# Running the products and the convolution of v ahead of q and k in the first stage of a two-layer attention kernel

## The chip, the core and the metric

The kernel runs on one core of a Trainium2 chip. A core has five engines with an instruction stream each: TensorE (PE in the profile, its weight loads PEld), VectorE (DVE), ScalarE (ACT), GpSimd (POOL) and SyncE (SP), which issues the DMAs of this kernel's first two stages. Each stream runs its instructions in the order in which the kernel was built, and semaphores make one stream wait for another. The metric is the device time of one execution, in microseconds (us).

## What is computed

The input x has 4 images of 192 channels and 128 x 128 pixels, in fp32. Two layers follow each other. The first is channel attention (8 heads of 24 channels, q and k divided by their norms over the pixels) with a gate:

```python
qkv = dwconv3x3(conv1x1(x, w_qkv), w_dw)
q, k, v, l = jnp.split(qkv, 4, axis=1)
attn = softmax(einsum('bhcn,bhdn->bhcd', q, k) * temperature)
out = einsum('bhcd,bhdn->bhcn', attn, v)
pooled = mean(l, axis=(2, 3))
t = conv1x1(relu(conv1x1(pooled, w_fc1, b_fc1)), w_fc2, b_fc2)
L = t * sigmoid(t)
out = conv1x1(L + out + x, w_proj) + L
```

The second is a dilated local attention: x gains a depthwise 3x3 convolution and a bias, a 1x1 convolution gives q, k and v, six heads of 32 channels attend to 9 neighbours at a dilation of 1, 2 or 3, and a 1x1 convolution follows. Its code is not touched by the change.

## The kernel before

There are three stages, one after the other.

**First stage** (`project`, `plan_projection`). The images go in pairs, and a pair in 32 blocks of four rows, so there are 64 blocks n. A block's x (`xt`, 128 partitions by 3 by 512 elements: 128 channels of each image, and the 64 remaining channels of both) is loaded by three DMAs. Its 1x1 convolution gives q and k in three tiles of 128 channels (`mt` 0 to 2) and v in tile 3 and a `shared` tile for the last 64 channels of both images. A tile of q and k takes full-array products (L293) and then products of the 64 remaining channels on two halves of the array (L298); v takes L426, L431, L303 and, on half the columns, L307. The results stand in `pu`, six buffers of PSUM, until ScalarE copies them out: q and k to `us` (six buffers, L311), which a DMA stores to `qk_dram` (L315); v to `vboth` and `ring` (L322), which hold three blocks of rows. Every third block some rows are copied again behind a ring's end (L172).

The depthwise convolution of v is done on these rings. For the first 128 channels ScalarE makes the centre tap into `pa` (one buffer, L333), and VectorE adds eight taps to it (L340), of which the last writes `v_False`. For the shared tile ScalarE makes nine scaled copies (centre L333, and `side`, three buffers, L352), which GpSimd sums (L363). Both are stored to DRAM (L370, L373). VectorE also sums every block of x for the gate (`totals`, L377), and GpSimd copies its edge columns (`edges`, L381).

The order of all this is made by hand and by a small planner (`Schedule`). Each operation is added with an engine, a rank, a cost and what it must follow; `order()` plays the plan through, and on every free engine takes the ready operation of the lowest rank, with a small penalty where a product would change the shape of the array. `hold` says how long a buffer is taken. Ranks are in blocks: rank n is the time of block n. SyncE's DMAs are planned the same way, and its stream, too, is fixed in that order: a store that waits for its data holds back all DMAs behind it. The weights of later stages are given ranks from 8 on.

**Second stage** (`channel_attention`). For each of 8 heads, first for q and then for k (`convolved`, `which` 0 and 1), the depthwise convolution is made by products with band matrices (L576) in six steps of four channels. A step loads `band` (three buffers, L555; GpSimd completes it, L563 and L566) and `u` (four buffers, four DMAs each from `qk_dram`, L558). ScalarE copies the results out of `pc` (L585), VectorE takes their statistics (L589). Then come the products of q and k (L648) and the rest of the head. At the end of each of the six steps `step()` is called (L590), which runs the next piece of pending work on small tiles: first the two gates (`gate_bias`, five pieces each for a pair of images), then the softmax of the heads done. The gate's products go to a PSUM buffer, and the head's results to a buffer in SBUF, that lie where the first stage had its own.

**Third stage** (`second_pass`): the product with the mixed weights, and the second layer. It takes most of the time.

The change touches `plan_projection` (ranks in `plan_products` and `plan_conv`), one line of `project`, and the call of `step()` in `convolved`.

Of the kernel before, what the change touches and what calls it, by code (L numbers as in the profile page):

```python
# [24 lines left out]
RING = 12  # L25
# [161 lines left out]
FULL, COLS, ROWS, QUADS = "128x128", "128x64", "64x128", "128x32"  # L187
# [64 lines left out]
def project(tc, x, load, other_loads, sums, qk_dram, v_dram, v2_dram):  # L252

    nc = tc.nc
    with ExitStack() as ctx:
        wts = ctx.enter_context(tc.tile_pool(name="p1w", bufs=1))
        wx, wx2, wv2, dwv = (load(wts, n) for n in ("wx", "wx2", "wv2", "dwv"))
        stage = Stage(ctx, tc, "p1", dict(xt=4, us=6, v=3, v2=3, side=3, ring=1), dict(pu=6, pa=1))  # L260
        rings = stage.pools["ring"]
        vboth = rings.tile([128, RING + SPARE, 2, W + 2], F32, tag="vboth", name="vboth")
        ring = [vboth[:, :, 0], vboth[:, :, 1]]
        ring.append(rings.tile([128, RING + SPARE, W + 2], F32, tag="ring2", name="ring2"))
        for r in ring:
            nc.gpsimd.memset(r[:, :, 0 : W + 2 : W + 1], 0.0)
        plan_projection(nc, stage, x, wx, wx2, wv2, dwv, vboth, ring, sums, qk_dram, v_dram, v2_dram)
        for i, run in enumerate(other_loads):
            stage.schedule.add("SP", 8 + i, 0.5, run)
        stage.run(tc)  # L270


def plan_projection(nc, stage, x, wx, wx2, wv2, dwv, vboth, ring, sums, qk_dram, v_dram, v2_dram):
# [113 lines left out]
        nc.vector.tensor_reduce(sums[n // NB][2][:, :, to : to + 1], tiles["xt", n][:, :, of : of + W], AX.X, ALU.add)  # L387

    def plan_products(n):
        load_op = add("SP", n - 1.5, 0.5, (loads, n), latency=6.0)  # L390
        users = []
        shared = add("PE", n + 0.52, 0.86, (shared_tile, n, 0), [load_op], FULL)
        users.append(shared)
        for mt in range(4):
            t = n + 0.5 * (mt // 2) + 0.01 * (mt % 2)
            first, second = (first_half_v, second_half_v) if mt == 3 else (first_half, second_half)
            args = (n,) if mt == 3 else (n, mt)
            a = add("PE", t, 1.72, (first, *args), [load_op], FULL)
            b = add("PE", t + 0.2, 0.86, (second, *args), [a], ROWS)
            users += [a, b]  # L400
            if mt == 3:
                continue
            evs = [add("ACT", t + 0.25, 0.56, (qk_evict, n, mt, im), [b]) for im in range(2)]
            for ev in evs:
                hold("pu", a, ev)
            hold("us", evs[0], add("SP", t + 0.3, 0.3, (qk_store, n, mt), evs, latency=5.0))
            evs[1]["first"].append(evs[0])
        last = add("PE", n + 0.75, 0.9, (shared_tile, n, 1), [shared], COLS)
        users.append(last)
        for m in range(3):  # L410
            ev = add("ACT", n + 0.8, 0.56, (v_evict, n, m), [last if m == 2 else b])
            stage.fill("u", m, n, RING, ev)
            stage.repeat(ring, "u", m, n, RING, n + 0.83)
            hold("pu", shared if m == 2 else a, ev)
        users.append(add("DVE", n + 0.5, 1.7, (totals, n), [load_op]))
        users += [add("POOL", n + 0.3 * k, 0.2, (edges, n, k), [load_op]) for k in range(3)]
        if n % NB == 0:
            users.append(add("DVE", n, 0.5, (edge_row, n, 2, 0), [load_op]))
        if n % NB == NB - 1:
            users.append(add("DVE", n, 0.5, (edge_row, n, 0, PX - W), [load_op]))  # L420
        hold("xt", load_op, *users)
# [9 lines left out]
            mm(tiles["pu", n, 3, im], w, tiles["xt", n][HALVES[im], 2, :], start=False, stop=True)  # L431

    def plan_conv(n):
        prev = first = add("ACT", n + 2, 1.2, (centre, n, False), latency=0.3)
        for j, t in enumerate(AROUND):
            prev = add("DVE", n + 2 + (j + 0.9) / 8, 1.22, (tap, n, t, j == 7), [prev])
            for m in range(2):
                stage.read("u", m, n, t // 3 - 1, prev)
        for m in range(2):
            stage.read("u", m, n, 0, first)  # L440
        hold("pa", first, prev)
        store = add("SP", n + 3.0, 0.3, (v_store, n, False), [prev], latency=5.0)
        hold("v", prev, store)
        prev = first = add("ACT", n + 2, 0.7, (centre, n, True))
        stage.read("u", 2, n, 0, first)
        for j, t in enumerate(AROUND):
            sd = add("ACT", n + 2 + (j + 0.4) / 8, 0.68, (side, n, t))
            stage.read("u", 2, n, t // 3 - 1, sd)
            prev = add("POOL", n + 2 + (j + 0.9) / 8, 1.26, (side_sum, n, t), [sd, prev])
            hold("side", sd, prev)  # L450
        store = add("SP", n + 3.0, 0.3, (v_store, n, True), [prev], latency=5.0)
        hold("v2", first, store)

    for n in range(2 * NB + 1):
# [64 lines left out]
def channel_attention(tc, d, load, qk_dram, mix1, mix2, band_p, u_p, gates):  # L519
# [7 lines left out]
    with ExitStack() as ctx:  # L527
# [18 lines left out]
        def convolved(hd, which, pool):  # L546
            c0 = which * C + hd * CH0
            full = pool.tile([128, B, W // 4, CH0, 4], F32, tag="conv", name=f"conv{which}_{hd}")
            stats = st.tile([128, B, CH0, 6], F32, tag=f"stats{which}", name=f"stats{which}_{hd}")
            for c2 in range(0, half, 2):  # L550
                band = band_p.tile([128, 2, 2, 3, G], F32, tag="band", name=f"band{which}_{hd}_{c2}")
                u = u_p.tile([128, 2, 2, B * W], F32, tag="u", name=f"u{which}_{hd}_{c2}")
                for e in range(2):
                    first = c0 + e * half + c2
                    nc.sync.dma_start(band[HALVES[e], e], d["bands"][:, first : first + 2])  # L555
                    for r in range(2):
                        to = (r + e) % 2 * G
                        nc.sync.dma_start(  # L558
                            u[to : to + G, e],
                            qk_dram[first : first + 2, r * G : (r + 1) * G].rearrange("c h b w -> h c (b w)"),  # L560
                        )
                for e in range(2):
                    nc.gpsimd.tensor_copy(band[HALVES[1 - e], e], band[HALVES[e], e])  # L563
                    for r in range(2):
                        cut = G - 1 - r * (G - 1)
                        nc.gpsimd.memset(band[HALVES[(r + e) % 2], e, :, :, cut : cut + 1], 0.0)  # L566
                for c in range(2):
                    pcs = [
                        ps_c.tile([128, B, W], F32, tag="pc", name=f"pc{which}_{hd}_{c2}_{c}_{e}") for e in range(2)
                    ]  # L570
                    for dx in (1, 0, 2):
                        to, of = shifted(dx)
                        for e in range(2):
                            for r in range(2):
                                at = slice((r + e) % 2 * G, (r + e) % 2 * G + G)
                                nc.tensor.matmul(  # L576
                                    pcs[e][r * G : (r + 1) * G, :, to],
                                    band[at, e, c, dx, :],
                                    u[at, e, c, :].rearrange("p (b w) -> p b w", w=W)[:, :, of],
                                    start=dx == 1,  # L580
                                    stop=dx == 2,
                                )
                    for e in range(2):
                        ch = e * half + c2 + c
                        nc.scalar.copy(full[:, :, :, ch, :], pcs[e].rearrange("p b (v w) -> p b v w", w=4))  # L585
                        for b in range(B):

                            of = pcs[e][:, b, :] if hd or which else full[:, b, :, ch, :]
                            nc.vector.bn_stats(stats[:, b, ch, :], of)  # L589
                step()  # L590

            flat = stats.rearrange("p b c s -> p (b c) s")
            sq = st.tile([128, B, CH0], F32, tag=f"sq{which}", name=f"sq{which}_{hd}")
            sqf = sq.rearrange("p b c -> p (b c)")
            nc.vector.tensor_mul(flat[:, :, 1:5:3], flat[:, :, 1:5:3], flat[:, :, 1:5:3])
            nc.vector.tensor_add(sqf, flat[:, :, 1], flat[:, :, 4])
            nc.vector.tensor_scalar_mul(sqf, sqf, float(W // 2))
            nc.vector.tensor_add(sqf, sqf, flat[:, :, 2])
            nc.vector.tensor_add(sqf, sqf, flat[:, :, 5])
            return full, sq  # L600
# [775 lines left out]
```

## Time and profile before

| | us |
|---|---|
| median of 3 runs (4567.59 to 4570.33) | 4569.71 |
| profiled execution | 4564.56 |
| its span | 4562.7 |
| first stage, to TensorE's last product of it | about 853 |
| second stage | to about 1630 |

The busy time of each engine in stretches of 100 us from the first stage's steady part to its end and into the second (TensorE, VectorE, ScalarE, GpSimd, and the granted clock of TensorE):

| stretch | TensorE | VectorE | ScalarE | GpSimd | clock |
|---|---|---|---|---|---|
| 600 to 700 | 100.00 | 88.84 | 87.71 | 78.85 | 1.00 |
| 700 to 800 | 100.00 | 91.83 | 87.66 | 81.41 | 1.00 |
| 800 to 900 | 81.88 | 81.51 | 72.65 | 67.28 | 0.91 |
| 900 to 1000 | 100.00 | 52.00 | 31.49 | 17.32 | 1.00 |

A row of the profile's groups or of its timeline names the line of the kernel, the engine, the operation, what it writes and reads, and how often; the bracket behind it gives the idle time before it and what ended that. Matmuls are pipelined and their ends are modelled, so the distance from one start to the next says more than their durations.

### The profile page before, as it was taken

The page shows a single profiled execution, that of the slowest core. Times are in us where ns is not written, and L with a number is a line of the kernel's source. Part 1 is how long each engine was busy: PE and PEld are TensorE (multiplying, and loading weights), DVE is VectorE, ACT ScalarE, POOL GpSimd, SP SyncE. Part 2 cuts the span into 40 slices and gives each one's busy share as a digit, 9 for nine tenths or more (in the row PEclk, how much of TensorE's full clock was granted, in tenths as well). Part 3 has the DMA queues.
Part 4 walks back from the last instruction along what each step waited for, and adds up shares of the span by engine and source line. Part 5 has one row for each costly group of instructions (what it writes and reads, how often), then busy time and mean ns, then how long its engine had stood idle before and what let it go on. Part 6 is the DMA issues. An engine that isn't in the chain of part 4 may idle for free.

```text
span 4562.7 us, 64190 instructions
## 1 busy us (share of the span) xinstructions
PE 4416.8 (97%) x20608; PEld 1602.8 (35%) x20608; DVE 3907.4 (86%) x5556; ACT 2506.2 (55%) x4794; POOL 3354.2 (74%) x3343
## 2 busy tenths in 40 slices
PE   9999999899999989999999999999999999999986
PEld 3333333345544532333333333333333333333321
DVE  7998889755455547899999999999999999999996
ACT  7888888633233345555555555555555555555531
POOL 6777788611111115888989999998998989999897
PEclk9999999999999989999999999999999999999997
DMA  8777787678677734443444443444434444344311
GB/s 271 241 242 232 244 256 242 192 164 178 150 167 169 167 89 97 99 99 97 101 98 93 105 103 91 106 96 101 101 90 108 98 100 101 92 109 99 78 44 28
DMA packets 483951, 608.93 MB, mean 133 GB/s; under 512 B 136528, under 2 KB 318364, under 8 KB 483616
## 3 DMA queue, kind: packets, MB, share of 16 engines
q1 hardware_dynamic: 464160, 504.94, 40.6%
q0 software_dynamic: 19456, 99.89, 11.3%
q8 instruction: 166, 2.72, 0.3%
q14 instruction: 169, 1.38, 0.1%
HBM read 277.72 MB, written 201.33 MB: 105 GB/s over the span
## 4 chain that ended last, share of the span: by engine, by line
PE 71%; DVE 14%; issue 6%; POOL 6%; DMA 2%; ACT 1%; POOLq 0%; SPq 0%; DVEq 0%; ACTq 0%
PE pc L576 11%; PE ph L803 9%; PE pu L293 7%; PE ex L1146 6%; PE sc L1022 6%; DVE prod L1011 5%; DVE term L1152 5%; POOL acc L1155 4%; PE pu L298 4%; PE gram L648 4%; PE po L1168 3%; PE po L1164 3%; PE pkv L945 3%; PE pu L426 2%; PE q L1000 2%
## 5 line engine op out<-in xcount | busy, mean ns | idle before, releaser
L1155 POOL TENSOR_TENSOR acc<-acc,term 128x512 f32<-128x512 f32 x1536 | 1977.4, 1289 | 211.9 <-DVE term L1152 135.5
L1152 DVE TENSOR_TENSOR term<-ex,vring 128x512 f32<-128x512 f32 (+2 forms) x1596 | 1007.3, 661 | 65.8 <-PE ex L1146 38.9
L1011 DVE TENSOR_TENSOR prod<-q,kring 128x1536 f32<-128x1536 f32 (+1 forms) x600 | 1008.3, 1686 | 31.7 <-ACT kring L963 13.8
L363 POOL TENSOR_TENSOR v_True<-v_True,side 128x512 f32<-128x512 f32 (+1 forms) x512 | 647.9, 1267 | 168.8 <-ACT side L352 141.1
L340 DVE SCALAR_TENSOR_TENSOR pa<-vboth,dwv,pa 128x1024 f32<-128x1024 f32 (+1 forms) x448 | 574.3, 1282 | 76.8 <-ACT pa L333 54.3
L1146 PE MATMUL ex<-e_sb,spread 108*128 108x512 bf16 x1728 | 596.2, 387 | 45.2 <-DVE acc L1152 21.3
L858 DVE SCALAR_TENSOR_TENSOR pa<-hboth,posw,pa 128x1024 f32<-128x1024 f32 (+1 forms) x384 | 489.5, 1275 | 59.0 <-ACT pa L846 45.1
L576 PE MATMUL pc<-u,band 64*64 64x508 f32 (+1 forms) x4608 | 517.5, 590 | 1.4 <-ACT ring L322 1.4
L563 POOL COPY band<-band 64x384 f32<-64x384 f32 x192 | 96.7, 504 | 561.3 <-DMA band<-in_bands 484.8
L1022 PE MATMUL sc<-prod,pick 128*32 128x512 f32 x3456 | 484.1, 607 | 4.1 <-DVE e L1079 2.8
L589 DVE BATCH_NORM_STATS2 stats<-pc 128x6 f32<-128x128 f32 x1440 | 303.3, 283 | 141.3 <-ACT conv L585 141.1
L1146 PEld LDWEIGHTS <-spread 108*128 108x128 bf16 x1728 | 149.0, 98 | 723.7 <-issue 692.2
L945 PE MATMUL pkv<-y,wkv 128*128 128x512 f32 x768 | 389.0, 618 | 8.1 <-ACT kring L958 2.5
L882 ACT ACTIVATE side<-hring,posw 128x512 f32<-128x512 f32 x512 | 335.2, 710 | 102.1 <-DMA side<-side 79.8
L803 PE MATMUL ph<-xv,mix 128*128 128x512 f32 (+1 forms) x1024 | 383.4, 606 | 5.4 <-DMA xv<-v_dram 4.9
L585 ACT COPY conv<-pc 128x512 f32<-128x512 f32 x384 | 211.4, 587 | 295.4 <-PE pc L576 288.8
L293 PE MATMUL pu<-xt,wx 128*128 128x512 f32 x768 | 365.3, 612 | 7.6 <-DMA xt<-in_x 7.6
L352 ACT ACTIVATE side<-ring,dwv 128x512 f32<-128x512 f32 (+1 forms) x512 | 350.6, 736 | 15.1 <-POOL v_True L363 14.3
L958 ACT COPY kring<-pkv 64x512 f32<-64x512 f32 x384 | 223.2, 581 | 221.7 <-PE pkv L948 210.5
L576 PEld LDWEIGHTS pc<-u,band 64*64 64x64 f32 x4608 | 188.4, 133 | 302.3 <-issue 282.1
L1171 ACT COPY o<-po 128x512 f32<-128x512 f32 x192 | 106.2, 588 | 304.5 <-PE po L1164 203.8
L958 ACT COPY vring<-pkv 64x512 f32<-64x512 f32 x384 | 223.4, 582 | 45.4 <-PE pkv L948 35.7
(164 smaller groups left out, 5961.0 us busy)
## 6 DMA issues: line engine op xcount, KB each, us to landing
qk_dram<-us SPq DMA_DIRECT2D x192, 512.0 KB
u<-qk_dram SPq DMA_DIRECT2D x384, 256.0 KB
side<-side POOLq DMA_DIRECT2D x124, 768.0 KB, 5.8
xt<-in_x SPq DMA_DIRECT2D x64, 512.0 KB
v_dram<-v_False SPq DMA_DIRECT2D x64, 512.0 KB
xv<-in_x SPq DMA_DIRECT2D x128, 256.0 KB
xv<-v_dram SPq DMA_DIRECT2D x128, 256.0 KB
out<-o SPq DMA_DIRECT2D x128, 256.0 KB
```

The lines of the kernel that those rows point to most:

```text
L293: mm(pu, wx[:, mt * 128 : (mt + 1) * 128], tiles["xt", n][:, im, :], start=True, stop=False)
L340: nc.vector.scalar_tensor_tensor(by_row(to[:, o : o + length]), by_row(vboth[:, at : at + length, :, t % 3 : t % 3 + W]), dwv[:, 0, t : t ...
L363: nc.gpsimd.tensor_add(v[:, rows, :], v[:, rows, :], z[:, rows, :])
L576: nc.tensor.matmul(pcs[e][r * G : (r + 1) * G, :, to], band[at, e, c, dx, :], u[at, e, c, :].rearrange("p (b w) -> p b w", w=W)[:, :, of], ...
L803: mm(to, w[:, cols], tiles["xv", n, j, im], start=j == 0, stop=j == 2)
L858: nc.vector.scalar_tensor_tensor(by_row(to[:, o : o + length]), by_row(hboth[:, at : at + length, :, t % 3 : t % 3 + W]), posw[:, 0, t : t ...
L945: mm(rows3(tile_of("pc", key)), w, tiles["y", n, im], start=True, stop=False)
L1011: nc.vector.tensor_mul(to[:, :, px].rearrange("p t (r w) -> p t r w", w=W), q.unsqueeze(1).to_broadcast([128, 3, *q.shape[1:]]), three,)
L1022: mm(sc[quad * 32 : (quad + 1) * 32, :], pick[:, QR - 4 * row : QR - 4 * row + 32], tiles["prod", n, k // NT, k % NT // 3][:, k % 3, :], s ...
L1146: mm(rows3(tile_of("ex", ("ex", n, g, t))), spread[:, t, :], e_sb, start=True, stop=True)
L1152: nc.vector.tensor_mul(rows3(to[:, px]), rows3(ex[:, px]), win)
L1155: nc.gpsimd.tensor_add(tiles["acc", n, g], tiles["acc", n, g], tiles.pop(("term", n, g, t)))
```

## The change

In the ranks of the first stage the load of x moves from n - 1.5 to n - 4.0 and gets seven buffers instead of four. v's products (tile 3 and the shared tile), their evictions and the convolution of v move three blocks earlier: products from n + 0.5 to n - 2.5, convolution from n + 2 to n - 1. Tile 0 of q and k moves from n to n - 0.5, tile 1 from n + 0.01 to n, tile 2 from n + 0.5 to n + 0.01. The totals and the edges keep their ranks. In the second stage the steps of the first head's q no longer call `step()`, so the gates' pieces begin with its k.

```diff
--- before.py
+++ after.py
@@ -257,7 +257,7 @@
     with ExitStack() as ctx:
         wts = ctx.enter_context(tc.tile_pool(name="p1w", bufs=1))
         wx, wx2, wv2, dwv = (load(wts, n) for n in ("wx", "wx2", "wv2", "dwv"))
-        stage = Stage(ctx, tc, "p1", dict(xt=4, us=6, v=3, v2=3, side=3, ring=1), dict(pu=6, pa=1))
+        stage = Stage(ctx, tc, "p1", dict(xt=7, us=6, v=3, v2=3, side=3, ring=1), dict(pu=6, pa=1))
         rings = stage.pools["ring"]
         vboth = rings.tile([128, RING + SPARE, 2, W + 2], F32, tag="vboth", name="vboth")
         ring = [vboth[:, :, 0], vboth[:, :, 1]]
@@ -387,12 +387,12 @@
         nc.vector.tensor_reduce(sums[n // NB][2][:, :, to : to + 1], tiles["xt", n][:, :, of : of + W], AX.X, ALU.add)
 
     def plan_products(n):
-        load_op = add("SP", n - 1.5, 0.5, (loads, n), latency=6.0)
+        load_op = add("SP", n - 4.0, 0.5, (loads, n), latency=6.0)
         users = []
-        shared = add("PE", n + 0.52, 0.86, (shared_tile, n, 0), [load_op], FULL)
+        shared = add("PE", n - 2.48, 0.86, (shared_tile, n, 0), [load_op], FULL)
         users.append(shared)
         for mt in range(4):
-            t = n + 0.5 * (mt // 2) + 0.01 * (mt % 2)
+            t = n + (-0.5, 0.0, 0.01, -2.49)[mt]
             first, second = (first_half_v, second_half_v) if mt == 3 else (first_half, second_half)
             args = (n,) if mt == 3 else (n, mt)
             a = add("PE", t, 1.72, (first, *args), [load_op], FULL)
@@ -405,12 +405,12 @@
                 hold("pu", a, ev)
             hold("us", evs[0], add("SP", t + 0.3, 0.3, (qk_store, n, mt), evs, latency=5.0))
             evs[1]["first"].append(evs[0])
-        last = add("PE", n + 0.75, 0.9, (shared_tile, n, 1), [shared], COLS)
+        last = add("PE", n - 2.25, 0.9, (shared_tile, n, 1), [shared], COLS)
         users.append(last)
         for m in range(3):
-            ev = add("ACT", n + 0.8, 0.56, (v_evict, n, m), [last if m == 2 else b])
+            ev = add("ACT", n - 2.2, 0.56, (v_evict, n, m), [last if m == 2 else b])
             stage.fill("u", m, n, RING, ev)
-            stage.repeat(ring, "u", m, n, RING, n + 0.83)
+            stage.repeat(ring, "u", m, n, RING, n - 2.17)
             hold("pu", shared if m == 2 else a, ev)
         users.append(add("DVE", n + 0.5, 1.7, (totals, n), [load_op]))
         users += [add("POOL", n + 0.3 * k, 0.2, (edges, n, k), [load_op]) for k in range(3)]
@@ -431,24 +431,24 @@
             mm(tiles["pu", n, 3, im], w, tiles["xt", n][HALVES[im], 2, :], start=False, stop=True)
 
     def plan_conv(n):
-        prev = first = add("ACT", n + 2, 1.2, (centre, n, False), latency=0.3)
+        prev = first = add("ACT", n - 1, 1.2, (centre, n, False), latency=0.3)
         for j, t in enumerate(AROUND):
-            prev = add("DVE", n + 2 + (j + 0.9) / 8, 1.22, (tap, n, t, j == 7), [prev])
+            prev = add("DVE", n - 1 + (j + 0.9) / 8, 1.22, (tap, n, t, j == 7), [prev])
             for m in range(2):
                 stage.read("u", m, n, t // 3 - 1, prev)
         for m in range(2):
             stage.read("u", m, n, 0, first)
         hold("pa", first, prev)
-        store = add("SP", n + 3.0, 0.3, (v_store, n, False), [prev], latency=5.0)
+        store = add("SP", n, 0.3, (v_store, n, False), [prev], latency=5.0)
         hold("v", prev, store)
-        prev = first = add("ACT", n + 2, 0.7, (centre, n, True))
+        prev = first = add("ACT", n - 1, 0.7, (centre, n, True))
         stage.read("u", 2, n, 0, first)
         for j, t in enumerate(AROUND):
-            sd = add("ACT", n + 2 + (j + 0.4) / 8, 0.68, (side, n, t))
+            sd = add("ACT", n - 1 + (j + 0.4) / 8, 0.68, (side, n, t))
             stage.read("u", 2, n, t // 3 - 1, sd)
-            prev = add("POOL", n + 2 + (j + 0.9) / 8, 1.26, (side_sum, n, t), [sd, prev])
+            prev = add("POOL", n - 1 + (j + 0.9) / 8, 1.26, (side_sum, n, t), [sd, prev])
             hold("side", sd, prev)
-        store = add("SP", n + 3.0, 0.3, (v_store, n, True), [prev], latency=5.0)
+        store = add("SP", n, 0.3, (v_store, n, True), [prev], latency=5.0)
         hold("v2", first, store)
 
     for n in range(2 * NB + 1):
@@ -587,7 +587,8 @@
 
                             of = pcs[e][:, b, :] if hd or which else full[:, b, :, ch, :]
                             nc.vector.bn_stats(stats[:, b, ch, :], of)
-                step()
+                if hd or which:
+                    step()
 
             flat = stats.rearrange("p b c s -> p (b c) s")
             sq = st.tile([128, B, CH0], F32, tag=f"sq{which}", name=f"sq{which}_{hd}")
```

## The prediction

> **What bounds the kernel now.** I read the page first: TensorE's busy share leads, so the question for a stage is whether TensorE ever waits in it.
>
> ```profile
> span 4562.7 us, 64190 instructions
> PE 4416.8 (97%) x20608; PEld 1602.8 (35%) x20608; DVE 3907.4 (86%) x5556; ACT 2506.2 (55%) x4794; POOL 3354.2 (74%) x3343
> ```
>
> Then the timeline of TensorE at the end of the first stage. The columns are start, busy time, engine, line, operation, names, and in brackets idle time and what ended it.
>
> ```profile
> 786.92 3.70 PE L293 MATMUL pu<-xt,wx 128*128 128x512 f32 x8
> 790.55 1.99 PE L298 MATMUL pu<-xt,wx 64*128 64x512 f32 x8
> 792.47 1.98 PE L293 MATMUL pu<-xt,wx 128*128 128x512 f32 x4
> 794.38 1.13 PE L298 MATMUL pu<-xt,wx 64*128 64x512 f32 x4
> 795.44 1.98 PE L426 MATMUL pu<-xt,wx 128*128 128x512 f32 x4
> ...
> 839.97 3.70 PE L293 MATMUL pu<-xt,wx 128*128 128x512 f32 x8
> 843.60 1.99 PE L298 MATMUL pu<-xt,wx 64*128 64x512 f32 x8
> 845.52 1.98 PE L293 MATMUL pu<-xt,wx 128*128 128x512 f32 x4
> 847.34 1.88 PE L426 MATMUL pu<-xt,wx 128*128 128x512 f32 x4
> ...
> 851.92 1.08 PE L307 MATMUL pu<-xt,wx 128*64 128x512 f32 x4
> 854.46 8.12 PE L576 MATMUL pc<-u,band 64*64 64x512 f32 x72 [1.45 <-ACT ring L322]
> 878.98 0.46 PE L489 MATMUL pl<-reach,wl 128*96 128x9 f32 x2 [16.41 <-DVE v_False L340]
> ```
>
> Rows begin where the last ends: TensorE bounds the stage. The first block shown takes 13.36 us (its successor starts at 800.28), the last 12.96. The first returns to the 64-row shape once more: two extra changes of array shape, 0.40 us, 0.20 each. The products end at 852.93. Then TensorE idles 1.45 and 16.41 us, the second until VectorE's last tap of block 63. That idle is the prize. VectorE's and GpSimd's timelines show the tail:
>
> ```profile
> 857.22 9.24 DVE L340 SCALAR_TENSOR_TENSOR pa<-vboth,dwv,pa 128x1024 f32<-128x1024 f32 x7 [4.33 <-ACT pa L333]
> 869.08 8.44 DVE L340 SCALAR_TENSOR_TENSOR pa<-vboth,dwv,pa 128x1024 f32<-128x1024 f32 x7 [1.30 <-ACT pa L333]
> 877.55 1.28 DVE L340 SCALAR_TENSOR_TENSOR v_False<-vboth,dwv,pa 128x1024 f32<-128x1024 f32 x1
> ...
> 873.03 7.18 POOL L363 TENSOR_TENSOR v_True<-v_True,side 128x512 f32<-128x512 f32 x6
> ```
>
> After the last product of v, two blocks of convolution remain: VectorE ends 25.9 us later (878.83), GpSimd 27.3 (about 880.2).
>
> **What the Trainium skill says.** "TensorEngine Tiling (Array Packing)", Key Properties: changing the tiling mode drains TensorE. The trace agrees, 0.20 us a change. "TensorE: Matmul & The Clock Gate", section on the architectural detail of the array: ScalarE and VectorE are strict FIFOs, and only weight loads are pulled ahead on TensorE. It agrees: convolution products stood behind L489 for 16.41 us. "DMA: Bandwidth & Descriptors", Two DMAs through the same engine are not ordered: a dependent DMA must wait for the first one's semaphore. SyncE's waits show this, u (L558) for the q store: 1.6 us, once.
>
> **The change, part by part.** It adds no arithmetic; the built instruction order shows what moves. Times below count from the end of the last product of v, "V".
>
> *End of the stage.* Behind V the changed order still has q's and k's tiles 1 and 2 (of three, 128 channels each) of block 61 and all three of 62 and 63: three pair groups of 5.55 us (839.97 to 845.52) and two single groups of 2.97 (792.47 to 795.44), 22.6 us. VectorE's tail hangs on the eviction of v, the centre tap and 16 taps in one accumulator; nothing in it shortens, so it ends at V + 25.9. The first gate products (L489) now stand ahead of the head's products and wait for it: 25.9 - 22.6 = 3.3 us idle instead of 1.45 + 16.41 = 17.9. Gain 14.6. The 72 products that ran at 854.46 now run after it, at the same cost.
>
> SyncE is next in line. Its order puts both stores of v of block 63 ahead of the rest of u. GpSimd's tail without the two band copies that stood in it (871.27 to 873.03) is 25.5 us; evictions now mixed between `side` copies add some 0.7, so V + 26.2. Two issues take 1.1 (1.09 at 880.24), the u load 0.6, and landing 4.9 (the first x, 2.60 to 7.48): V + 32.8. TensorE needs it after the gate's 2.9 and 16 products of 0.22, at V + 32.4. Cost 0.4, from 0 (a landing of 3.9, as one x at 388.80) to 3. The other u parts follow 1.2 us apart, a tile per 5.35.
>
> *Shapes.* Of the products' rows, 369 neighbours differ in shape in the order before, 403 in the new one: pair, single and v groups interleave worse. 34 x 0.20 = 6.8 us, all on TensorE, which bounds the stage. Bounds 5 to 8.
>
> *Start.* Before, block 3 ended at 63.79; four blocks of 12.96 from 7.61 end at 59.45, so 4.3 us were lost. Now SyncE loads seven x first, and GpSimd's edge copies of all seven stand ahead of its first side sum. Block landings at 8.6, 12.2, 15.4, 18.2 put the seventh at 18.2 + 3 x 3.1 = 27.5. The first sum ends at 29.0; ScalarE, with three `side` buffers, holds its fourth and fifth copy behind the first two sums and tile 0's evictions behind those, so tile 0's first accumulator comes free at 31.2. TensorE has done three blocks of v, tile 0 of block 0 and one product of tile 1 by 25.6 (7.61 + 4.84 + 4.84 + 7.41 + 0.9) and waits until 31.3. Sums then pace ScalarE until v of block 3 ends at 43.8, where unbroken work (two v groups of 4.84, 795.44 to 800.28, two merged ones of 7.41, 845.52 to 852.93, and a pair) would end at 37.7: lost 6.1, so + 1.8. Bounds -2 (x lands faster) to + 6.
>
> *DMA behind the start.* The same bytes, three x earlier. Weights (25 small loads) and the first stores come after them on SyncE, and the slices from 50 to 100 us already ran at 292 GB/s with the engines 94% busy. x is now needed four blocks after issue, and `us` frees six deep, so this should hide; if not, a late x holds GpSimd's edge copies, then ScalarE. 0 to 5 us, I take 1.
>
> *Seven buffers of x.* 18 KB more per partition; the head's buffer over it waits for the same last tap. Nothing, or up to 1.6 us gained where x was late (388.80).
>
> *Gate.* Six calls of step() leave q for k and the next head. The same products, about 11 us with their waits, run on TensorE either way: 0, bounds -1 to + 1.
>
> Sum: -14.6 + 0.4 + 6.8 + 1.8 + 1.0 = -4.6 us against the profiled execution, 4564.56 (span 4562.7 plus 1.9 around it), giving 4560.0. The median of the runs is 5.15 above that execution, so I forecast 4569.71 - 4.6 = 4565.1.
>
> **Rivals.** Against 0.2%, 9.1 us, which is about what a measurement here can tell from no change.
>
> (a) *The lead covers everything.* The start costs no more than before, u lands in time, no x is late: -14.6 + 6.8 - 1.6 = -9.4, and with a shorter tail (conv of 61 done earlier, since totals and gate sums no longer stand in it) -11: 4559. For it: VectorE and GpSimd have slack, 12.2 us (taps 10.5, total 1.7) and 10.6 (8 sums of 1.27 and the edges) in a block of 13.2. Against: the tail was already only taps.
>
> (b) *Slower: accumulators run short in every block.* v holds three of six `pu` buffers at a group's end, and ScalarE then stands before `pa`'s centre tap (L333) until VectorE is done, with q's and k's evictions queued behind. From V, evicting v takes 1.6, the ring copies 1.5 in every third block, side, centre and two more 3.8; k's evictions come at about 7 and the next v needs their buffers at 7.4 where its group merges with q's, at 8.5 otherwise. If the centre waits over 0.5 to 1 us longer than now, TensorE loses the rest. At 0.3 us in 60 blocks that is 18 us: 4583. For it: ScalarE is 88% busy here (87.66 of 100 us at 700 to 800). Against: before has the same counts of buffers and evictions and TensorE waits 3.3 us in all. It decides from 0.23 us a block.
>
> (c) *Not what it says.* The head's start moves less than the products do, because u waits behind the v stores and the side sums end late (V + 31): the net is about 0, 4570.
>
> **How the numbers follow.** Forecast's own case 0.50 (4561 to 4569), (a) 0.20, (b) 0.17, (c) 0.13. Faster by over 0.2% is (a), 0.20; slower (b), 0.17; the rest 0.63. The range 4556 to 4578 takes in (c), most of (a) and the upper bounds of start, backlog and landing (+ 4.2, + 4, + 2.6), and leaves out most of (b).
>
> **What would show it.** Right: TensorE idle at L489 of 2 to 5 us on VectorE's last tap; the products ending some 9 us later than 852.93; a first long wait near 27 to 31 us; more of the rows with two 64-row groups. Wrong: TensorE waits on ScalarE spread over the whole stage (b), a wait on u's DMA of over 3 us (c), or an idle below 1 us at L489 with the products ending before 860 (a).

## The result

| | median us | lowest to highest | runs |
|---|---|---|---|
| kernel before | 4567.28 | 4564.25 to 4570.58 | 20 |
| changed kernel | 4575.35 | 4568.62 to 4577.77 | 20 |

The changed kernel takes 1.0017 times as long, with a 95% interval of 1.001 to 1.0024. It is 8.1 us slower where 4.6 us less was forecast. The two profiled executions differ by a similar amount, 9.8: 4574.39 against 4564.56, spans 4572.6 and 4562.7. The changed kernel's page has:

```profile
span 4572.6 us, 64232 instructions
PE 4438.0 (97%) x20608; PEld 1605.8 (35%) x20608; DVE 3910.5 (86%) x5556; ACT 2511.8 (55%) x4795; POOL 3359.3 (73%) x3343
```

TensorE has as many instructions as before, but 21.2 us more of busy time (4416.8 before). About half of that was forecast, as 14.6 us less idle time in a total only 4.6 us shorter. The rest of the loss does not appear as idle time either. A product of k's convolution is shown with 586 to 641 ns, and in an unbroken step the products overlap so far that 48 take 5.35 us. When data is late fewer overlap: the row becomes longer (6.37 us below), and TensorE counts as busy all through it.

The timeline of TensorE in the changed kernel, from the end of the first stage through head 0, to the start of head 1's products of q and k. The gram product is L649 here and was L648 before.

```profile
859.56 1.99 PE L298 MATMUL pu<-xt,wx 64*128 64x512 f32 x8
864.73 0.34 PE L489 MATMUL pl<-reach,wl 128*96 128x9 f32 x2 [3.18 <-DVE v_False L340]
...
867.40 38.19 PE L576 MATMUL pc<-u,band 64*64 64x512 f32 x288
907.07 6.57 PE L576 MATMUL pc<-u,band 64*64 64x512 f32 x48 [1.49 <-DMA cut<-qk_dram]
914.25 6.37 PE L576 MATMUL pc<-u,band 64*64 64x512 f32 x48 [0.60 <-DMA u<-qk_dram]
920.78 6.37 PE L576 MATMUL pc<-u,band 64*64 64x512 f32 x48 [0.16 <-POOL band L566]
...
927.71 6.37 PE L576 MATMUL pc<-u,band 64*64 64x512 f32 x48 [0.39 <-POOL band L566]
...
941.44 5.35 PE L576 MATMUL pc<-u,band 64*64 64x512 f32 x48
946.73 0.34 PE L489 MATMUL pl<-reach,wl 128*96 128x9 f32 x2
...
954.22 1.43 PE L649 MATMUL gram<-conv,conv 128*96 128x96 f32 x14
1050.28 1.43 PE L649 MATMUL gram<-conv,conv 128*96 128x96 f32 x14
```

Up to 867.40 the two sizes that were forecast are met: the products of the first stage end at 861.55 (call this moment P; it was 853.00 before), and the wait at L489 is 3.18 us, forecast 3.3. Then q's 288 products take 38.19 us, although 48 of them unbroken take 5.35, so 32.1 for 288: 6.1 us are lost inside a row without a bracket (part of them by a slower clock, see the last section). In k, four of the six steps take 6.37 to 6.57 instead of 5.35, with waits of 0.16 to 1.49 between them. And at 946.73, with k's convolution over, products of the second gate are still owed.

What TensorE's weight loads wait for in this stretch (862 to 950) says more than the brackets of the products; columns are total us, times, longest:

```profile
PEld pc L576 <- POOL band L566: 7.7, 8, 2.4
```

GpSimd completes a band when its load has landed, and the DMA engines are nearly always full while k runs. Busy time in stretches of the changed kernel; the last three columns are TensorE's clock, the DMA engines' busy share, and GB/s:

```profile
900.00:910.00 10.00, 8.51 (x68) 4.59 (x65) 6.88 (x29) 3.20 (x6) 1.61 (x6) 1.00 1.03 228
910.00:920.00 10.00, 9.40 (x79) 5.26 (x72) 5.10 (x24) 3.68 (x7) 1.41 (x6) 1.00 0.95 206
920.00:930.00 10.00, 9.46 (x73) 4.91 (x73) 5.24 (x25) 3.35 (x6) 2.82 (x12) 1.00 1.00 218
930.00:940.00 10.00, 10.00 (x91) 4.54 (x83) 5.32 (x26) 5.08 (x9) 2.83 (x12) 1.00 1.07 220
```

A step needs four u loads of 256 KB and two of band of 96 KB, 1.245 MB. At 218 GB/s, the mean of the four rows, that is 5.7 us, more than the 5.35 that the step's products take, and the rows of `cut` come on top. So in k the loads set the pace, once the stock of u is used up. They could have been further ahead: earlier in head 0 the DMA engines stood still for some 5 us, because SyncE, with the next loads behind it in its stream, waited for one of the three band buffers. The second fence is from SyncE's waits between 850 and 925; columns are total us, times, longest.

```profile
876.00:878.00 2.00, 2.00 (x12) 0.75 (x9) 0.00 (x0) 0.56 (x1) 0.00 (x0) 1.00 0.12 30
878.00:880.00 2.00, 2.00 (x18) 0.85 (x19) 0.88 (x4) 0.03 (x1) 0.00 (x0) 1.00 0.00 0
```

```profile
SPq L555 <- PE pc L576: 7.9, 3, 7.1
```

In the kernel before, that stock was filled up to and during the 17.9 us in which TensorE idled. By 878.98, when TensorE went on, SyncE had issued 19 loads of u, almost five tiles, of which one and a half were used; in the changed kernel it had issued nine by 867.40, when the first products ran. For the last 8 us or so of the idle time the DMA engines of the kernel before stood still as well, while SyncE waited at a store of v (L373) for GpSimd's last sums (9.7 us at the longest); one row of the same view of before:

```profile
870.00:880.00 10.00, 1.02 (x6) 1.00 (x6) 8.59 (x8) 4.19 (x8) 9.18 (x13) 0.50 0.20 51
```

### The profile page after: what moved, and what is told of

It reads as the page before. It is cut to its first block, busy times and chain, and to the rows that moved or that the text cites. A ratio compares the mean times of both kernels' runs of the same rounds, so it can differ in the third digit from the quotient of the medians.

```text
span 4572.6 us, 64232 instructions
## 1 busy us (share of the span) xinstructions
PE 4438.0 (97%) x20608; PEld 1605.8 (35%) x20608; DVE 3910.5 (86%) x5556; ACT 2511.8 (55%) x4795; POOL 3359.3 (73%) x3343
## 4 chain that ended last, share of the span: by engine, by line
PE 71%; DVE 14%; issue 5%; POOL 5%; DMA 3%; ACT 1%; SPq 0%; POOLq 0%; DVEq 0%; ACTq 0%
PE pc L576 11%; PE ph L804 9%; PE pu L293 7%; PE ex L1147 7%; PE sc L1023 6%; DVE prod L1012 6%; DVE term L1153 5%; PE pu L298 4%; PE gram L649 4%; POOL acc L1156 4%; PE po L1169 3%; PE po L1165 3%; PE pkv L946 3%; PE pu L426 2%; PE q L1001 2%
## 5 line engine op out<-in xcount | busy, mean ns | idle before, releaser
L585 ACT COPY conv<-pc 128x512 f32<-128x512 f32 x384 | 212.5, 587 | 309.8 <-PE pc L576 301.4
L352 ACT ACTIVATE side<-ring,dwv 128x512 f32<-128x512 f32 (+1 forms) x512 | 352.6, 736 | 10.6 <-POOL v_True L363 6.2
```

## The experiments

TensorE's position in the one profiled execution of each kernel shows more than the medians, whose difference is uncertain by some 3 us. P differed by 3.4 us among the eight runs with the changed kernel's order in the first stage (860.6 to 864.0), and the time from head 7's gram to the end by 9 (2958.3 to 2967.3), where no kernel here differs from another. So I compare the time from P to the start of head 1's gram. (The expectations below call P "the last product of v"; the numbers in them are counted from P as it is defined here.) All the medians stand beside runs of the kernel before on the same chip.

| kernel | P | P to head 1's gram | median minus before, us | ratio, 95% interval |
|---|---|---|---|---|
| before | 853.0 | 190.2 | | |
| changed | 861.6 | 188.7 | +8.1 | 1.001 to 1.0024 |
| gate edit alone | 852.1 | 191.5 | +0.9 | 0.9993 to 1.0009 |
| lead of v alone | 861.2 | 180.2 | -1.6 | 0.9991 to 1.0004 |
| changed, few u | 863.6 | 180.1 | -1.4 | 0.999 to 1.0007 |
| before, few u | 852.1 | 190.2 | -2.5 | 0.9986 to 1.0002 |
| lead, few u | 863.6 | 180.5 | -2.3 | 0.9989 to 1.0005 |
| lead without gate | 864.0 | 180.8 | +0.9 | 0.9994 to 1.001 |
| lead without gate, few u | 861.7 | 169.6 | -8.1 | 0.9975 to 0.9989 |
| changed, SyncE eased | 860.9 | 185.4 | +5.6 | 1.0001 to 1.0017 |
| lead, SyncE eased | 860.6 | 181.1 | -1.7 | 0.9989 to 1.0006 |
| lead, tiles together | 855.6 | 185.2 | -4.9 | 0.9983 to 0.9996 |
| the same, stores of v on GpSimd | 856.0 | 181.2 | -10.6 | 0.9966 to 0.9985 |
| before, tiles together | 851.7 | 191.9 | -4.5 | 0.9983 to 0.9996 |

### The change in two parts

The gate edit alone, on the kernel before:

```diff
-                step()
+                if hd or which:
+                    step()
```

> The kernel before with the gate edit alone (steps begin with the first head's k). Theory S (supply: head 0 is short of u because the idle of before, in which u was fetched, is gone): no lead of v, so the tail of v's convolution still holds head 0; the gate products no longer stand in front, but the six accumulators fill after 72 products and their evictions wait for the memory that the last v tiles leave. Before 0 to +3 us. Rival G (the gate edit itself costs the 8 us, its steps crowding into k): before +6 to +9 us.

The lead alone is the changed kernel with this edit undone.

> The changed kernel with the gate's steps left where they were (from the first head's q on). S: head 0 is still short of u, so as the changed kernel: before +6 to +10 us. G: the loss goes, before -5 to 0 us.

Measured: +0.9 and -1.6 us. Neither part alone costs anything that can be told in the total; together they cost 8. My theory S, in the form it had then, put the lead alone at +6 to +10 and was wrong; the rival G put the gate edit alone at +6 to +9 and was wrong, too. What is left is an interaction. The lead alone on TensorE:

```profile
867.29 22.71 PE L576 MATMUL pc<-u,band 64*64 64x512 f32 x144
889.93 0.25 PE L498 MATMUL pf<-pool,fc1T 96*12 96x2 f32 x4
890.11 5.35 PE L576 MATMUL pc<-u,band 64*64 64x512 f32 x48
...
901.10 1.79 PE L515 MATMUL pb<-gate,eye 96*128 96x1 f32 x16
902.82 5.35 PE L576 MATMUL pc<-u,band 64*64 64x512 f32 x48
...
929.38 15.60 PE L576 MATMUL pc<-u,band 64*64 64x512 f32 x144
944.91 3.66 PE L618 MATMUL pcut<-cut,cuttaps 96*48 96x512 f32 x12
```

The first 144 products are late here as well (22.71 instead of 16.05), but from 890 on all steps run unbroken, with the gate's products between them. The convolution of k ends at 944.9 with the gate done; in the changed kernel it ends at 946.7 with gate products still to come. That gave a second theory: the loads set when the convolution of head 0 can end, and the gate's products cost nothing as long as they run while u is being fetched.

### Fewer loads

In head 0, q and k each load one tile of u and of band and use it for all six steps, so that 10 of its 12 pairs of loads are gone. The products stay.

```diff
-                band = band_p.tile([128, 2, 2, 3, G], F32, tag="band", name=f"band{which}_{hd}_{c2}")
-                u = u_p.tile([128, 2, 2, B * W], F32, tag="u", name=f"u{which}_{hd}_{c2}")
-                for e in range(2):
+                if hd or not c2:
+                    band = band_p.tile([128, 2, 2, 3, G], F32, tag="band", name=f"band{which}_{hd}_{c2}")
+                    u = u_p.tile([128, 2, 2, B * W], F32, tag="u", name=f"u{which}_{hd}_{c2}")
+                for e in range(2 if hd or not c2 else 0):
```

> The changed kernel, but head 0 loads one tile of u and one of band for q and one of each for k and uses them for all six steps: 10 of its 12 u and band loads are left out, so its values differ; TensorE's products are as many. S: only the first tile can be late, so of the 12 to 13 us lost in head 0 some 7 to 12 come back: before -4 to +1 us, and after the first tile no 48 products take over 5.6 us. Rival H (the loss lies in the first stage, shapes and start, not in head 0): as the changed kernel, before +6 to +9 us.

> The kernel before with the same loads of head 0 left out (its values differ in the same way). S: its head 0 was not short of u, so nothing to gain: before -2 to 0 us. H says nothing of it. If it gains as much as the changed kernel does (7 or more), u costs both the same and S falls.

> The lead alone, with 10 of the 12 u and band loads of head 0 left out as in the two runs above (its values differ). S2: only the first tile can be late, q's 144 first products take under 20 us, and little else is to be had since the gate's products filled the other waits: before -6 to -2, that is within 3 us of the changed kernel with the same loads left out. G2: 7 to 9 us below that one.

The changed kernel gains 8.6 us from P to head 1's gram (188.7 to 180.1), and its median is 1.4 us under the kernel before, which is no difference that can be told. The kernel before and the lead alone gain nothing there (190.2 and 190.2, 180.2 and 180.5). With few loads it no longer matters where the gate stands: 180.1 in k, 180.5 in q. The DMA's share in the changed kernel with few loads, while k runs, is the other side of it:

```profile
900.00:910.00 10.00, 10.00 (x100) 4.02 (x96) 7.21 (x32) 4.69 (x8) 0.67 (x3) 1.00 0.14 37
910.00:920.00 10.00, 10.00 (x100) 3.96 (x96) 7.61 (x37) 4.65 (x8) 0.79 (x4) 1.00 0.41 92
```

One number did not fit: q's first 144 products still took 22.88 us in the lead with few u (expected under 20). That early loss is not the later tiles, which were not loaded there. What is left is the first tile, whose second halves are issued behind the stores of v, and TensorE's clock (see the last section).

### Without the gate

```diff
+        gates = []
+        for bias in biases:
+            nc.gpsimd.memset(bias, 0.0)
         channel_attention(tc, d, load, qk_dram, mix1, mix2, band_p, u_p, gates)
```

> The lead without the gate's products, sums after them and sigmoid (the 12 steps of two pairs of images; the bias is set to zero instead, so the values differ): about 11 us of TensorE's time are left out. With no steps the changed kernel and the lead alone are the same kernel. Theory S3: head 0 is paced by the bytes of u and band, which the DMA brings at 200 to 220 GB/s, so in the lead alone most of those 11 us were free: from the last product of v to head 1's gram 176 to 181 us (lead alone 180.2, changed kernel 188.7), and by the time before -6 to 0. Rival: TensorE's products add up: 169 us or less, before -13 to -9.

> The lead without the gate's products and with 10 of the 12 u and band loads of head 0 left out (both parts make its values differ). S3, in which the loads hid the gate's 11 us: without them TensorE paces head 0 and the 11 us come off, from the last product of v to head 1's gram 168 to 173 us (180.8 with all loads, 180.5 with the gate and few loads), before -14 to -8. If it stays at 178 or more, something other than the loads paced head 0 and S3 falls.

These two runs take the gate's products off the lead and set its bias to zero. Taking the 11 us off changes nothing: 180.8 us to head 1's gram against 180.2. By the median it is +0.9, slightly outside the -6 to 0 expected, with a P 2.8 us later than in the lead alone. With few loads as well, the 11 us come off: 169.6, median -8.1. So the gate's products were free in the lead, and it was the loads that made them free. A small part may be the clock's: without the gate's products TensorE's waits of 1.77 and 2.02 us (below) were each followed by 3.4 us at half clock, from 910.2 and 930.7, which by themselves are worth at most 3.4 us. The timeline of the lead without the gate shows the rhythm of the loads with nothing in between:

```profile
876.55 30.95 PE L579 MATMUL pc<-u,band 64*64 64x512 f32 x256 [0.20 <-DMA u<-qk_dram]
909.27 19.12 PE L579 MATMUL pc<-u,band 64*64 64x512 f32 x144 [1.77 <-POOL band L569]
930.41 17.93 PE L579 MATMUL pc<-u,band 64*64 64x512 f32 x144 [2.02 <-POOL band L569]
```

With few loads the same products run almost unbroken (64.0 us for 574 at 5.35 per 48):

```profile
867.03 67.79 PE L580 MATMUL pc<-u,band 64*64 64x512 f32 x574 [1.44 <-DMA u<-qk_dram]
```

Three stretches of the same traces show how the two parts of the change work on each other: from P to the end of k's convolution in head 0 (the next product of another kind), from there to head 0's gram, and from there to head 1's gram.

| kernel | P to the end of k's convolution | to head 0's gram | to head 1's gram |
|---|---|---|---|
| before | 93.7 | 3.6 | 92.9 |
| gate edit alone | 88.0 | 7.5 | 96.0 |
| lead of v alone | 83.7 | 3.6 | 93.0 |
| changed | 85.2 | 7.5 | 96.1 |
| lead, few u | 83.7 | 3.6 | 93.2 |
| changed, few u | 76.5 | 7.5 | 96.1 |
| lead without gate | 84.2 | 3.6 | 93.0 |
| lead without gate, few u | 73.0 | 3.6 | 93.0 |

Wherever the gate edit is in, some 7 us stand behind the convolution of k: 3.9 before head 0's gram, where the second gate's first products divide those of `pcut`, and 3.1 in head 1, where its last pieces run. In return the convolution ends 5.7 us earlier on the kernel before, and 7.2 earlier with few loads. With the lead and all loads it ends no earlier (85.2 against 83.7), since with all loads it takes 84.2 us even when the gate's products are left out altogether, and 73.0 only with few loads.

### SyncE's order

In the changed kernel the second halves of the first u tiles stand behind the stores of v of block 63, then SyncE waits at 872.8 for a band buffer until 880.00, and later it loads eight small constants. SyncE's timeline there:

```profile
863.19 0.63 SPq L558 DMA_DIRECT2D u<-qk_dram  x1
863.87 1.14 SPq L315 DMA_DIRECT2D qk_dram<-us  x2
865.10 1.19 SPq L370 DMA_DIRECT2D v_dram<-v_False  x1
866.38 2.54 SPq L373 DMA_DIRECT2D v_dram<-v_True  x2
868.97 3.85 SPq L558 DMA_DIRECT2D u<-qk_dram  x5
880.00 0.50 SPq L555 DMA_DIRECT2D band<-in_bands  x1
```

Three edits ease it, first on the changed kernel, then on the lead alone: the stores of v of block 63 go out through GpSimd's queue, the band loads follow the u loads of their step, and the constants follow k's loads.

```diff
+        queue = nc.gpsimd if n == 2 * NB - 1 else nc.sync
...
                 for e in range(2):
                     first = c0 + e * half + c2
-                    nc.sync.dma_start(band[HALVES[e], e], d["bands"][:, first : first + 2])
                     for r in range(2):
...
+                for e in range(2):
+                    first = c0 + e * half + c2
+                    nc.sync.dma_start(band[HALVES[e], e], d["bands"][:, first : first + 2])
...
             q, sq = convolved(hd, 0, q_p)
+            k, sk = convolved(hd, 1, k_p)
             if hd == 0:
                 same, same_row, fold, fold_rows, ones, ident, wph, tempr = (
                     load(wts, n) for n in "same same_row fold fold_rows ones ident wph temp".split()
                 )
-            k, sk = convolved(hd, 1, k_p)
```

> The changed kernel, whole, with SyncE's order eased in three places: the stores of v of block 63 go out from GpSimd, the eight small constants are loaded after k's loads instead of between q's and k's, and each tile's u loads stand ahead of its band loads. Theory S2 (head 0 of the lead is paced by the loads of u, and the gate's products are free only while they fill those waits): q and k of head 0 together lose under 6 us to waits instead of 12 to 13, so 5 to 9 us come back: before -2 to +3. Rival G2 (the gate's steps in k cost 8 us with the lead whatever the loads do, by accumulators, VectorE or the order on TensorE): before +6 to +9.

> The same easing on the lead alone (gate's steps from q on). S2: the 6 to 7 us lost in q's first three tiles (22.71 instead of 16.05) go down to 1 to 3: before -8 to -4. G2 and a third reading (u's bytes at the DMA's full rate are the limit, whatever the order of issue): before -3 to 0.

The changed kernel gains 3.3 us (188.7 to 185.4) and stays 5.6 above before, outside what S2 expected; k's steps with 6.37 us are still there. The lead gains nothing (181.1), as its third reading had it: there the order of issue, as eased here, is not the limit. Whether the limit is the bytes of u, the arrival of band, which most of the waits of k name, or the number of buffers, these runs do not separate: the loads were left out together, and no run has a fourth band buffer. SyncE waits for a band buffer here too, 5.8 us at the longest in the changed kernel and 6.3 in the lead.

### Fewer shape changes, and a faster kernel

The three tiles of q and k get ranks beside each other, on the lead (shown) and on the kernel before (0.0, 0.01, 0.02 and 0.5):

```diff
-            t = n + (-0.5, 0.0, 0.01, -2.49)[mt]
+            t = n + (0.0, 0.01, 0.02, -2.49)[mt]
```

> The lead alone with q's and k's three tiles of a block ranked together, so that the built order has 320 changes of array shape among the first stage's products instead of 403. If each costs 0.20 us and nothing else moves, the products end 83 x 0.20 = 17 us earlier than in the lead alone: before -19 to -14. Rival: a group of three pairs fills all six accumulators, the next v waits for ScalarE's evictions, 0.5 us or more in each of 64 blocks: before +14 and up.

> The kernel before (v in its old place, four buffers of x, gate in q) with q's and k's three tiles ranked together: 320 changes of array shape among the first stage's products instead of 369. At 0.20 us each the products end 49 x 0.20 = 10 us earlier, less what the accumulators cost (in the lead some 7 of 17 us): before -10 to -3. If slower, the grouping needs the lead.

> The lead with q's and k's three tiles ranked together (which gave before -4.9), and the stores of v of block 63 sent from GpSimd's queue, so that the second halves of the first four u need not stand behind them on SyncE. If the place in the queue matters: from the last product of v to head 0's gram 92.3 goes down to 86 to 90, before -11 to -7. If the bytes alone matter (S3): 91 to 93, before -7 to -3.

With the lead, a block in the steady part then has five groups of one shape, and no wait on the accumulators: two blocks follow each other in 12.96 us (402 to 428, TensorE):

```profile
401.86 5.42 PE L293 MATMUL pu<-xt,wx 128*128 128x512 f32 x12
407.20 2.85 PE L298 MATMUL pu<-xt,wx 64*128 64x512 f32 x12
409.98 1.98 PE L426 MATMUL pu<-xt,wx 128*128 128x512 f32 x4
...
414.82 5.42 PE L293 MATMUL pu<-xt,wx 128*128 128x512 f32 x12
```

P comes 5.6 us earlier than in the lead alone, a third of the 17 expected. The price of a change is not what failed: of the stage's 2432 products, the 1900 behind the first 380 take 648.2 us instead of 661.4 (counted in the traces), 13.1 less for 66 fewer changes, or 0.20 each. The start takes it back: the first 380 end 7.5 us later, and TensorE waits 6.8 us for ScalarE within the first 60 us (3.3 in the lead alone). Then 5 us are given back before head 1's gram, 185.2 instead of 180.2: P is earlier, and the u loads behind the stores of v are not. With block 63's stores of v on GpSimd's queue 4 of these come back (181.2, and 88.3 to head 0's gram, within what was expected if the place in the queue matters). Here, then, the order of issue does count. How much of the 4 us is the clock is open: after P it was at half for 13.7 us in the first of the two kernels and for 6.8 in the second. The second kernel has a median of 4557.81, 10.6 us under the kernel before (interval 0.9966 to 0.9985) and so faster than the kernel before, where the changed one was slower. Up to head 7's gram its trace shows 6.0 of them (1597.4 against 1603.4); where the others lie is not shown. The kernel before gains 4.5 by the grouping, too, but its one profiled execution is 4.4 above its median and shows none of it.

## Why the prediction was wrong

Its sum, term by term, in the profiled executions:

| term | forecast | measured |
|---|---|---|
| P (shapes 6.8, start 1.8) | +8.6 | +8.6 |
| late x behind the start | +1.0 | no wait on x after the first block |
| P to head 1's gram, the lead's share (-14.6, u +0.4) | -14.2 | -10.0 |
| P to head 1's gram, the gate edit's share | 0 | +8.5 |
| head 1's gram to head 7's | 0 | -1.3 |
| from there to the end | 0 | +4.1 |
| sum | -4.6 | +9.9 |

*The step that failed* is the one on the gate: "The same products, about 11 us with their waits, run on TensorE either way: 0, bounds -1 to + 1." It holds for a TensorE that never waits. In head 0 of the lead the loads set the pace, and the gate's 11 us of work lie in waits for them at no cost, as the runs without the gate show. Moved to k and the next head they came on top: 8.5 us (188.7 against 180.2), of which 3.9 stand between k's convolution and head 0's gram, 3.1 in head 1 and 1.5 in the convolution itself, which the loads kept from ending earlier. They vanish when the loads are left out. On the kernel before the same edit costs 0.9 us by the median, no change that can be told: there the convolution became 5.7 us shorter in exchange, and leaving out loads gains nothing, so u was not short.

*The second miss* is a size in the lead itself: u's landing at 0.4, "from 0 to 3. The other u parts follow 1.2 us apart, a tile per 5.35". The lead's share came out 4.2 short. The second halves of u were issued at 868.97 behind the stores of v, as the step said. The later tiles are not it: in the lead the convolution takes 83.7 us with and without them. Nor is the clock, by much: at half for 6.8 us of the lead's products, against 5.6 in the kernel before, an estimated 0.6 us more. What remains is, most likely, the first tile, later than the step had it; no run changes it alone, so how these 3 to 4 us arise stays open. Behind both misses lies one omission: of the 17.9 us of idle that I called the prize, the DMA engines used the first part to fetch u, and the sum had no term for what that was worth.

*What held.* The idle at L489 (3.18 for 3.3), and P (+8.6), though the exact agreement is partly luck. Counted in the traces, the first 380 products end 5.8 us later with 13 more changes of shape; at 0.20 each that leaves 3 us for the start, where 1.8 was forecast. The next 1900 take 2.6 us more with 20 more changes, and a wait of 1.07 us that the kernel before had among them (at 410.66) is gone: 0.19 us a change. The start had a wrong detail, too: the long wait came at 41.7 and lasted 2.70 us, not at 25.6 with 5.7, and the clock fell to half for 3.4 us behind it. One reading was too strong: the products behind L489 did not wait for it alone in the kernel before. The six accumulators of `pc` were full after 72 products, and ScalarE's first copies out of them (L585, at 878.99) waited for the same last tap of VectorE. Rival (b) did not occur: from 60 us to P TensorE shows no wait on ScalarE. Rival (c) had the right direction, that u is late, but its reason, the place behind the stores, is worth at most 3 to 4 us of the 12.7: 3.3 in the changed kernel with SyncE eased, 4.0 with the tiles together, nothing in the lead. The row of +4.1 at the end of the table is within the 9 us by which that stretch scatters. I had listed a wait on u of over 3 us as the sign of (c); the brackets on the products show 2.6 us on DMA and band together. The loss stood in longer rows and in the weight loads' waits instead.

The range, 4556 to 4578, holds the time; the sign of the forecast is wrong.

## What to carry to other kernels

Before you count an engine's idle time as a gain, ask which transfers use it: take the bytes that the next part needs per step, divide by the rate that the trace shows with the DMA engines full, and compare with the step's time on the engine. Look, too, at where the DMA engines stand still, and for which buffer. Work that fills such waits is free where it stands and costs its full time where you move it to, so two edits that are harmless alone can cost together; test them apart and together. In a timeline, check the length of a row against its count, since a wait on data can hide in a row without a bracket.

## What was not expected of the hardware

TensorE's clock fell to half after an idle of only 3.2 us, and fell some 2 us after work had begun again, on the gate's small products. The lead alone, with the clock third from the end:

```profile
865.00:866.00 1.00, 0.73 (x7) 0.62 (x6) 0.17 (x1) 0.00 (x0) 0.12 (x1) 1.00 1.05 332
867.00:868.00 1.00, 1.00 (x5) 0.56 (x8) 0.53 (x3) 0.00 (x0) 0.00 (x0) 0.50 1.08 385
...
872.00:873.00 1.00, 1.00 (x5) 0.23 (x2) 0.00 (x0) 0.26 (x1) 0.00 (x0) 0.53 0.82 143
873.00:874.00 1.00, 1.00 (x8) 0.29 (x6) 0.65 (x4) 0.32 (x1) 0.00 (x0) 1.00 1.07 297
```

It was at half for 6.8 us here and for 3.4 in the changed kernel (0.89 at 866 to 867, 0.90 at 870 to 871). The Trainium skill, "TensorE: Matmul & The Clock Gate", Part 1, says that the clock halves after at least one idle window of about 3.4 us and rises after a busy one, with windows that run freely. One and two such windows agree with the lengths in these two runs. The idle time of 3.2 us is shorter than such a window, so here the clock fell without a whole idle one, unless a window of idle time and the gate's small products (9 columns each) counts as idle. The lead with SyncE eased is a case for that: there the clock fell at 909.6 with no idle time shown, after 3 us with hardly anything but such products. No run tests it.

Half clock for 6.8 us costs an estimated 3.4 us of the early loss, half of its length, and the prediction had not counted it. But it is not a difference from before: there the clock was at half, too, for the last 11.5 us of the idle time and the first 5.6 us of work behind it. Two rows of before:

```profile
882.00:884.00 2.00, 2.00 (x14) 0.50 (x9) 2.00 (x11) 0.02 (x1) 0.00 (x0) 0.50 0.78 217
884.00:886.00 2.00, 2.00 (x19) 0.71 (x12) 1.83 (x10) 0.23 (x1) 0.00 (x0) 0.86 0.74 249
```

The DMA engines were full (share 0.95 to 1.07) at 206 to 228 GB/s with u, band and `cut`, but moved 385 GB/s at 867 to 868, at a share of 1.08, with the last stores and first u loads. A full share therefore doesn't stand for one rate: the rate has to be read beside the transfers that make it up.
